# A two-layer graph transformer on one core: graphs taken in pairs, or singly with layer 0 of one beside layer 1 of the one in front

## Chip, core and metric

The kernel runs on one core of a Trainium2 chip. The metric is device time in microseconds. Three runs of the kernel before gave a median of 3158.67 us (3156.97 to 3158.88). A separate profiled execution has a span of 3156.3 us, and all readings of the trace refer to that span.

## What is computed

There are 32 graphs of 512 nodes with 256 features, in float32, each with a 512 x 512 integer adjacency. Two layers follow each other, both with 8 attention heads of 32 features:

```python
# layer 0
allowed = (adj > 0) | (adj.T > 0) | eye
h  = layernorm(x + attention(x, allowed) @ Wo.T + bo) * ln1_g + ln1_b
h  = layernorm(h + relu(h @ W1.T + b1) @ W2.T + b2) * ln2_g + ln2_b   # 256 -> 1024 -> 256
x2 = layernorm(x + h)
# layer 1
out = layernorm(x2 + attention1(x2, adj != 0) @ Wo1.T + bo1)
```

The graphs do not depend on each other. Within one graph everything is a chain.

## The kernel before, in words

One `Graph` object holds the tiles of a graph; its methods each issue a small piece of work, and `period` lists calls of these methods by hand. The order of the calls is the order of the instructions on every engine: the program is built without a scheduler, each engine works through its own queue in that order, and waits on semaphores where an operand or a buffer is not ready. `Absent` objects stand for graphs before the first and after the last: their methods do nothing.

The pieces that matter here:

- `scores` (L279): four matmuls of 32 contraction rows, one per head, into the only score buffer (`ps_s`, four PSUM banks), and the exponential on ScalarE into one of eight `p` tiles. A layer has eight such steps, k = 0 to 7: two head groups times four blocks of keys.
- `masked` (L293): VectorE multiplies `p` with the mask. `product` (L297): TensorE multiplies `p` with the values into 32 output columns a head; after the fourth of a head group ScalarE copies the result to `cT`.
- `pair` (L315) adds two `p` tiles by a DMA that GpSimd issues (p0 += p1, p2 += p3, p4 += p5); `fold` (L320) adds two on VectorE; `sums` (L328) lets TensorE add the folded tile over the keys; `divide` (L346) divides `cT` by it on VectorE, with two small additions on GpSimd in between.
- `project` (L389), then `out0` or `out1` (residual and statistics on VectorE), `root` (L369: add and power on GpSimd, two instructions), and `norm1` or `offset` and `norm4` (on ScalarE).
- The MLP works by halves of the nodes, h = 0 and 1: `hidden` (L408) four times, `mlp` (L434) twice, `out2`, `root(2)`, `norm2` (L446), `root(3)`, `norm3` (L452), which writes the rows of `x2`.
- `transpose` (L237) turns two blocks of 128 rows of `x`, `x1` or `x2` into `xT` through TensorE; `query_key` (L265) and `value` (L249) read `xT`.
- `cast` writes the adjacency to DRAM as bfloat16 (DMA from GpSimd); `entries` reads it back plain and transposed (DMAs from SP); `masks` (L213) makes both masks on VectorE; `load` and `again` bring `x` twice; `residual`, `residual1`, `residual2` add a row to a tile by DMA from GpSimd; `store` writes the result.

One call of `period` in the kernel before takes two graphs, c and d, through layer 0 and the next two steps of their life: first the second half of layer 1 of a pair in front (b's scores), then layer 0 of c, layer 0 of d beside the MLP of c, then layer 1 of c beside the MLP of d. Seventeen calls cover the 32 graphs.

Pools: `ps_d` gives three PSUM buffers in turn to everything but scores and products; products have one bank (`ps_a`); `work` has two buffers per tag unless a line says otherwise (`xT` one, `hT` one, `cT` one, `p` eight, `m1` four).

Of the kernel before, what the change touches and what calls it, by code (L numbers as in the profile page):

```python
# [11 lines left out]
I32 = mybir.dt.int32  # L12
AF = mybir.ActivationFunctionType
# [13 lines left out]
def kernel(ctx: ExitStack, tc: tile.TileContext, t: dict, out: bass.AP):  # L27
# [121 lines left out]
    def plain(pools: ExitStack):  # L149
# [26 lines left out]
        class Graph:  # L176


            def __init__(self, b):
                self.b = b  # L180
                self.mv, self.rs, self.pf = {}, {}, {}
# [7 lines left out]
            def load(self):  # L189
                nc.sync.dma_start(out=self.tile("x", [NQ, D]), in_=x[self.b].rearrange("(c p) d -> p c d", p=P))  # L190

            def again(self):

                nc.sync.dma_start(out=self.tile("x1", [NQ, D]), in_=x[self.b].rearrange("(c p) d -> p c d", p=P))

            def cast(self):

                self.code = hbm.tile([N, N], BF16, tag="code", name=f"code_{self.b}")
                nc.gpsimd.dma_start(
                    out=self.code.rearrange("(p c) k -> p (c k)", p=P),  # L200
                    in_=adj[self.b].rearrange("(p c) k -> p (c k)", p=P),
                )

            def entries(self):

                nc.sync.dma_start(
                    out=self.tile("m0", [NQ, N], BF16), in_=self.code.rearrange("(c p) k -> p c k", p=P)
                )
                self.tile("m1", [NQ, N], BF16, bufs=4)
                for i in range(NQ):  # L210
                    nc.sync.dma_start_transpose(out=self.m1[:, i, :], in_=self.code[:, i * P : (i + 1) * P])  # L211
# [9 lines left out]
            def once(self):  # L221

                if self.b == 0:
                    value_bias(0)
                    graphs[3].masks()
# [11 lines left out]
            def transpose(self, src, h):  # L237

                if h == 0:
                    self.tile("xT", [ND, N], bufs=1)  # L240
# [87 lines left out]
            def sums(self, k, hg, first=False, last=False):  # L328

                if first:  # L330
                    self.total = ps_d.tile([P, N], F32, tag="d", name=f"psR_{self.b}_{hg}")
# [4 lines left out]
                for i in beats:  # L336
                    for j in range(HPC):
                        nc.tensor.matmul(  # L338
                            self.total[j * HD : (j + 1) * HD, :],
# [6 lines left out]
            def divide(self, hg):  # L346
# [3 lines left out]
                nc.vector.transpose(sT.rearrange("p a b -> p (a b)"), self.total)  # L350
# [125 lines left out]
        graphs = [Absent()] * 2 + [Graph(b) for b in range(B)] + [Absent()] * 4  # L476

        def period(a, b, c, d, e, f):

            b.scores(1, 0)
            b.masked(1, 0)
            b.query_key(1, 0, 1)
            b.scores(1, 2)
            b.query_key(1, 1, 1)
            b.scores(1, 1)
            b.masked(1, 2)
            a.sums(3, 1, first=True, last=True)
            a.divide(1)  # L490
            b.product(0)
            d.load()
            c.transpose(c.x, 0)
            b.scores(1, 3)
            c.transpose(c.x, 1)
            a.project(1, 0)
            b.masked(1, 1)
            a.out1(0)
            b.scores(1, 5)
            b.masked(1, 3)  # L500
            b.masked(1, 5)
            a.out1(1)
            d.again()
            b.product(1)
            b.pair(0)
            b.product(2)
            b.scores(1, 4)
            a.project(1, 1)
            b.pair(2)
            a.out1(2)  # L510
            c.query_key(0, 1, 0)
            b.masked(1, 4)
            b.scores(1, 7)
            a.out1(3)
            c.query_key(0, 0, 0)
            b.masked(1, 7)
            b.product(3)
            b.scores(1, 6)
            b.fold(2, 2, 0)
            b.product(4)  # L520
            b.residual2()
            a.root(4, 0, 2)
            b.pair(4)
            c.query_key(0, 1, 1)
            b.masked(1, 6)
            a.root(4, 2, 4)

            c.scores(0, 0)
            b.fold(3, 6, 7)
            c.query_key(0, 0, 1)  # L530
            a.offset(0, 2)
            b.sums(2, 0, first=True, last=True)
            a.norm4(1)
            b.divide(0)
            c.scores(0, 1)
            b.fold(3, 3, 4)
            b.product(5)
            b.product(6)
            c.masked(0, 1)
            c.masked(0, 0)  # L540
            c.once()
            b.product(7)
            c.scores(0, 7)
            c.value(0, 0)
            c.residual()
            b.sums(3, 1, first=True, last=True)
            a.norm4(0)
            b.divide(1)
            c.scores(0, 2)
            c.value(0, 1)  # L550
            d.transpose(d.x, 0)
            c.scores(0, 3)
            c.product(0)
            c.masked(0, 2)
            b.project(1, 0)
            c.scores(0, 6)
            c.masked(0, 3)
            c.product(1)
            b.out1(0)
            a.offset(2, 4)  # L560
            c.product(2)
            d.transpose(d.x, 1)
            c.scores(0, 4)
            c.masked(0, 7)
            b.out1(1)
            c.masked(0, 6)
            c.pair(0)
            a.norm4(3)
            d.query_key(0, 1, 0)
            c.pair(2)  # L570
            c.masked(0, 4)
            c.scores(0, 5)
            c.masked(0, 5)
            a.norm4(2)
            d.query_key(0, 0, 0)
            b.project(1, 1)
            c.fold(2, 2, 0)
            c.product(3)

            d.scores(0, 0)  # L580
            c.once1()
            c.fold(3, 6, 7)
            b.root(4, 0, 2)
            b.offset(0, 2)
            b.out1(2)
            a.store()
            b.out1(3)
            c.product(4)
            c.pair(4)
            c.product(5)  # L590
            c.sums(2, 0, first=True, last=True)
            d.masked(0, 0)
            c.product(6)
            d.scores(0, 1)
            c.divide(0)
            c.fold(3, 3, 4)
            b.norm4(0)
            d.value(0, 0)
            c.product(7)
            d.scores(0, 2)  # L600
            d.query_key(0, 0, 1)
            d.query_key(0, 1, 1)
            d.scores(0, 3)
            b.root(4, 2, 4)
            b.norm4(1)
            d.product(0)
            c.sums(3, 1, first=True, last=True)
            b.offset(2, 4)
            d.masked(0, 1)
            d.masked(0, 2)  # L610
            d.product(1)
            b.norm4(2)
            b.norm4(3)
            c.divide(1)
            d.residual()
            d.masked(0, 3)
            d.scores(0, 4)
            d.value(0, 1)
            d.scores(0, 6)
            c.project(0, 0)  # L620
            c.project(0, 1)
            c.out0(0)
            d.pair(0)
            d.scores(0, 7)
            d.product(2)
            c.out0(1)
            c.root(1, 0, 2)
            c.norm1(0)
            c.norm1(1)
            c.out0(2)  # L630
            d.pair(2)
            d.product(3)
            c.out0(3)
            c.transpose(c.x1, 0)
            d.scores(0, 5)
            c.hidden(0, 0)
            c.hidden(0, 2)
            d.masked(0, 6)
            c.root(1, 2, 4)
            c.norm1(3)  # L640
            d.masked(0, 4)
            c.hidden(0, 4)
            c.norm1(2)
            c.hidden(0, 6)
            d.masked(0, 5)
            d.masked(0, 7)
            d.product(4)
            d.fold(3, 6, 7)
            d.fold(2, 2, 0)
            c.transpose(c.x1, 1)  # L650
            c.residual1()
            c.mlp(0)
            d.pair(4)
            c.mlp(1)
            c.out2(0)
            c.out2(1)
            c.hidden(1, 0)
            c.root(2, 0, 2)
            c.hidden(1, 2)
            c.hidden(1, 4)  # L660
            e.cast()
            c.hidden(1, 6)
            d.sums(2, 0, first=True, last=True)
            c.norm2(0)
            c.norm2(1)
            c.root(3, 0, 2)
            c.norm3(1)
            c.norm3(0)
            d.product(5)
            d.divide(0)  # L670
            c.transpose(c.x2, 0)
            d.fold(3, 3, 4)
            c.mlp(2)
            c.out2(2)
            c.mlp(3)
            c.root(2, 2, 3)
            c.norm2(2)
            d.product(6)
            c.root(3, 2, 3)
            d.sums(3, 1, first=True, last=True)  # L680
            c.out2(3)
            f.cast()
            d.product(7)
            c.norm3(2)
            c.value(1, 0)
            c.query_key(1, 1, 0, 0)
            e.entries()
            d.divide(1)
            f.entries()
# [329 lines left out]
```

## Time and profile before

The durations below are means over the whole execution, from the groups of the page. Instructions that follow each other directly overlap a little, so a row of them takes less than the sum.

| operation | line | engine | count | mean us |
|---|---|---|---|---|
| mask multiplication, p <- p, m | L295 | VectorE | 512 | 2.28 |
| fold, p <- p, p | L322 | VectorE | 189 | 2.29 |
| exponential | L290 | ScalarE | 512 | 1.88 |
| residual add, statistics (two instructions) | L385, L366, L367 | VectorE | 384, 512, 512 | 0.41, 0.43, 0.18 |
| transposes in `divide` | L350, L356 | VectorE | 256 | 0.71 |
| `norm3` | L454 | VectorE | 128 | 0.41 |
| `root`, add and power | L372, L373 | GpSimd | 320 each | 0.60, 0.89 |
| issue of `pair` (landing after 8.7 in the median) | L318 | GpSimd | 189 | 1.06 |
| scores | L286 | TensorE | 4096 matmuls | busy 584.8 in all |
| products | L303 | TensorE | 4096 matmuls | busy 510.4 in all |
| MLP, both steps | L417, L438 | TensorE | 4096 matmuls | busy 914.4 in all |

A float32 matmul shows as two instructions in the trace, a transpose as one. The text `32*128` behind a matmul gives the rows and columns of the array that it uses: scores use 32 rows (four heads side by side), products and sums 32 columns, all else the full 128 x 128.

### The profile page before, as it was taken

The numbers are of one execution on the slowest core, as the hardware profiler recorded it, in microseconds if no ns is written. First come the engines' busy times: TensorE is split into PE (matmuls) and PEld (weight loads), VectorE is DVE, ScalarE is ACT, GpSimd is POOL, SyncE is SP. The second block draws the span as 40 slices with busy tenths as digits, with TensorE's granted clock in tenths as the row PEclk, the third lists the DMA queues.
The fourth block names the chain that finished last, engine by engine and source line by source line (L and its number), as shares of the span: only waits on it lengthen the run. The fifth ranks groups of instructions, "written<-read, shape, count | busy, mean of one in ns | idle before, by whom it ended". The sixth has DMA issues, their size and how long they took to land.

```text
span 3156.3 us, 43843 instructions
## 1 busy us (share of the span) xinstructions
PE 3105.7 (98%) x17466; PEld 1751.6 (55%) x17466; DVE 2673.4 (85%) x3458; ACT 1683.5 (53%) x1921; POOL 895.4 (28%) x1254
## 2 busy tenths in 40 slices
PE   6999999999999999999999999999999999999998
PEld 2655637456474664746547465564655637456473
DVE  4889797897979879798897988979889798897977
ACT  4455464645646456464563645646455464554644
POOL 0232222332322323232232322322223222332322
PEclk8999999999999999999999999999999999999999
DMA  7656556664656647576465665656656556665633
GB/s 185 121 112 124 119 107 127 121 127 107 120 115 132 123 103 135 103 140 127 102 127 109 136 129 104 129 112 124 123 111 127 121 107 127 120 127 107 124 57 68
DMA packets 239876, 374.00 MB, mean 118 GB/s; under 512 B 80176, under 2 KB 214448, under 8 KB 214960
## 3 DMA queue, kind: packets, MB, share of 16 engines
q0 software_dynamic: 95824, 282.09, 49.2%
q1 hardware_dynamic: 143840, 89.03, 10.5%
q8 instruction: 139, 2.28, 0.3%
q14 instruction: 73, 0.60, 0.1%
HBM read 89.01 MB, written 33.55 MB: 39 GB/s over the span
## 4 chain that ended last, share of the span: by engine, by line
PE 89%; ACT 5%; DVE 3%; DMA 1%; SPq 1%; POOL 1%; issue 1%; POOLq 0%; DVEq 0%
PE psS L286 17%; PE psH L417 14%; PE psF L438 14%; PE psA L303 13%; PE psQK_None L273 8%; PE psV L256 6%; PE psO L397 6%; ACT p L290 5%; PE psR L338 4%; PE psQK L273 4%; PE psT L244 3%; DMA p<-p 1%; DVE st L366 1%; DVE x L381 1%; SPq L211 0%
## 5 line engine op out<-in xcount | busy, mean ns | idle before, releaser
L295 DVE TENSOR_TENSOR p<-p,m 128x2048 f32<-128x2048 f32 x512 | 1158.6, 2280 | 80.0 <-ACT p L290 78.2
L290 ACT ACTIVATE p<-psS 128x2048 f32<-128x2048 f32 x512 | 961.7, 1878 | 481.8 <-PE psS L286 379.8
L286 PE MATMUL psS<-qT,kT 32*128 32x512 f32 x4096 | 584.8, 641 | 11.1 <-ACT p L290 3.0
L303 PE MATMUL psA<-p,v 128*32 128x512 f32 x4096 | 510.4, 599 | 0.0
L417 PE MATMUL psH<-xT,w_L_gnn_W 128*128 128x256 f32 x2048 | 460.1, 381 | 0.0
L438 PE MATMUL psF<-w_L_gnn_W,hT 128*128 128x256 f32 x2048 | 454.3, 380 | 0.0
L322 DVE TENSOR_TENSOR p<-p,p 128x2048 f32<-128x2048 f32 x189 | 428.1, 2286 | 10.2 <-DMA p<-p 7.2
L417 PEld LDWEIGHTS psH<-xT,w_L_gnn_W 128*128 128x128 f32 x2048 | 383.9, 190 | 86.0 <-ACT xT L247 24.3
L438 PEld LDWEIGHTS psF<-w_L_gnn_W,hT 128*128 128x128 f32 x2048 | 384.1, 190 | 61.7 <-ACT hT L425 12.1
L372 POOL TENSOR_SCALAR rs<-mv 128x2 f32<-128x2 f32 (+1 forms) x320 | 190.8, 596 | 775.2 <-DVE mv L367 775.2
L425 ACT ACTIVATE hT<-psH,c_L_gnn_b 128x256 f32<-128x256 f32 x512 | 214.6, 470 | 285.9 <-PE psH L417 284.2
L286 PEld LDWEIGHTS psS<-qT,kT 32*128 32x128 f32 x4096 | 160.1, 183 | 312.3 <-issue 136.0
L318 POOL DMA_DIRECT2D p<-p x189 | 195.1, 1059 | 467.9 <-PE psA L303 295.0
L373 POOL TENSOR_TENSOR rs<-rs,neg_half 128x2 f32<-128x2 f32 (+1 forms) x320 | 286.1, 894 | 26.7
L303 PEld LDWEIGHTS psA<-p,v 128*32 128x32 f32 x4096 | 106.3, 109 | 314.9 <-issue 233.7
L273 PE MATMUL psQK_None<-xT,w_L_gnn_Wqkv 128*128 128x512 f32 x512 | 250.3, 618 | 4.7 <-DMA w_L_gnn_Wqkv<-in_L_gnn_Wqkv_dram 4.7
L397 PE MATMUL psO<-w_L_gnn_Wo,cT 128*128 128x256 f32 x1024 | 244.8, 384 | 0.7 <-DVE held L985 0.5
L397 PEld LDWEIGHTS psO<-w_L_gnn_Wo,cT 128*128 128x128 f32 x1024 | 187.9, 190 | 68.2 <-issue 40.6
L353 POOL TENSOR_TENSOR total<-total,sT 128x16 f32<-128x16 f32 x128 | 28.2, 221 | 654.1 <-DVE sT L350 645.1
L313 ACT COPY cT<-psA 128x512 f32<-128x512 f32 x128 | 74.9, 585 | 215.0 <-PE psA L303 206.7
L247 ACT COPY xT<-psT 128x512 f32<-128x512 f32 x192 | 112.1, 584 | 131.3 <-PE psT L244 131.1
L366 DVE BATCH_NORM_STATS2 st<-y 128x6 f32<-128x256 f32 x384 | 164.3, 428 | 13.1
(67 smaller groups left out, 2912.6 us busy)
## 6 DMA issues: line engine op xcount, KB each, us to landing
p<-p POOLq DMA_DIRECT2D x189, 1024.0 KB, 8.7
x<-in_x_dram SPq DMA_DIRECT2D x64, 512.0 KB, 5.3
x<-bov POOLq DMA_DIRECT2D x64, 512.0 KB, 5.8
code<-in_adj_dram POOLq DMA_DIRECT2D x32, 512.0 KB, 6.0
m<-code SPq DMA_DIRECT2D x32, 512.0 KB, 3.9
x<-s_L_gnn_ln_b POOLq DMA_DIRECT2D x32, 512.0 KB, 8.0
x<-s_L_gnn_b POOLq DMA_DIRECT2D x32, 512.0 KB, 6.0
out_dram<-x SPq DMA_DIRECT2D x32, 512.0 KB, 3.5
```

Source lines behind the costliest of these rows:

```text
L273: nc.tensor.matmul(ps, w[:, i, c * P : (c + 1) * P], self.xT[:, i, at], start=(i == 0), stop=(i == ND - 1))
L286: nc.tensor.matmul(s[:, j, :], self.kT[at, hg, kc * P : (kc + 1) * P], self.qT[at, hg, :], start=True, stop=True)
L290: nc.scalar.activation(p, s, AF.Exp, scale=SCALE)
L295: nc.vector.tensor_tensor(p, p, m[:, k % NQ, None, :].to_broadcast([P, HPC, N]), ALU.mult)
L303: nc.tensor.matmul(self.acc[hg][j * HD : (j + 1) * HD, :], self.v[:, kc, h * HD : (h + 1) * HD], self.p[k][:, j, :], start=(kc == 0), stop ...
L322: nc.vector.tensor_tensor(self.p[dst], self.p[a], self.p[b], ALU.add)
L366: nc.vector.bn_stats(st, y)
L373: nc.gpsimd.tensor_tensor(rs, rs, neg_half[:, a:b, None], ALU.pow)
L397: nc.tensor.matmul(ps[:, j, :], self.cT[:, k, at], wo[layer][:, k, :], start=(k == 0), stop=(k == ND - 1))
L417: nc.tensor.matmul(ps[:, j, :], w1[:, c, at], self.xT[:, c, h * 2 * P : (h + 1) * 2 * P], start=(c == 0), stop=(c == ND - 1),)
L425: nc.scalar.activation(self.hT[h][:, f + j, :], ps[:, j, :], AF.Relu, bias=b1[:, f + j : f + j + 1])
L438: nc.tensor.matmul(ps, self.hT[h][:, f, j * P : (j + 1) * P], w2[:, f, :], start=(f == 0), stop=(f == NF - 1))
```

## The change

The methods stay as they were, but for five small things: `load`, `again`, `cast` and `entries` do nothing if they ran before; `total` becomes a dictionary by head group, so that both sums of a graph can be open at once; `once` no longer calls `masks` of the second graph; `m1` has three buffers in place of four; `xT` has the pool's two in place of one.

The list in `period` is new. One call takes one graph on: layer 0 attention of c beside the second MLP half of b, then layer 1 attention of b beside the first MLP half of c, while a's last steps and d's first steps go between. 35 calls cover the 32 graphs. At the start the second x (twice) and its entries are issued on SP behind two weights, ahead of all other weights.

```diff
             def load(self):
-                nc.sync.dma_start(out=self.tile("x", [NQ, D]), in_=x[self.b].rearrange("(c p) d -> p c d", p=P))
+                if not hasattr(self, "x"):
+                    nc.sync.dma_start(out=self.tile("x", [NQ, D]), in_=x[self.b].rearrange("(c p) d -> p c d", p=P))
...
-                self.tile("m1", [NQ, N], BF16, bufs=4)
+                self.tile("m1", [NQ, N], BF16, bufs=3)
...
-                    graphs[3].masks()
...
-                    self.tile("xT", [ND, N], bufs=1)
+                    self.tile("xT", [ND, N])
...
-                    self.total = ps_d.tile([P, N], F32, tag="d", name=f"psR_{self.b}_{hg}")
+                    self.total[hg] = ps_d.tile([P, N], F32, tag="d", name=f"psR_{self.b}_{hg}")
...
-        graphs = [Absent()] * 2 + [Graph(b) for b in range(B)] + [Absent()] * 4
-        def period(a, b, c, d, e, f):
...
+        graphs = [Absent()] * 3 + [Graph(b) for b in range(B)] + [Absent()] * 4
+        def period(a, b, c, d, e):
+            a.product(7)
+            c.scores(0, 0)
+            a.fold(3, 6, 7)
+            c.masked(0, 0)
+            b.hidden(1, 0)
+            b.hidden(1, 4)
+            c.scores(0, 2)
+            a.fold(3, 3, 4)
+            b.hidden(1, 2)
+            c.product(0)
+            a.sums(3, 1, first=True, last=True)
+            a.divide(1)
+            c.masked(0, 2)
+            c.scores(0, 4)
+            b.hidden(1, 6)
+            a.project(1, 0)
+            a.out1(0)
+            a.out1(1)
+            c.scores(0, 1)
+            a.project(1, 1)
+            a.root(4, 0, 2)
+            a.out1(2)
+            a.out1(3)
+            c.masked(0, 4)
+            a.offset(0, 2)
+            b.mlp(3)
+            c.masked(0, 1)
+            a.norm4(1)
+            a.norm4(0)
+            c.scores(0, 3)
+            b.transpose(b.x2, 0)
+            c.once()
+            b.out2(3)
+            b.mlp(2)
+            c.scores(0, 5)
+            c.product(1)
+            c.product(2)
+            c.residual()
+            a.root(4, 2, 4)
+            c.pair(0)
+            b.root(2, 3, 4)
+            c.masked(0, 3)
+            b.out2(2)
+            c.product(3)
+            b.root(2, 2, 3)
+            c.scores(0, 6)
+            c.pair(2)
+            b.norm2(3)
+            b.query_key(1, 0, 0, 0)
+            b.norm2(2)
+            b.root(3, 3, 4)
+            b.root(3, 2, 3)
+            c.product(4)
+            b.norm3(3)
+            c.masked(0, 5)
+            b.norm3(2)
+            c.masked(0, 6)
+            c.scores(0, 7)
+            c.masked(0, 7)
+            c.fold(2, 2, 0)
+            c.fold(3, 6, 7)
+            a.offset(2, 4)
+            b.transpose(b.x2, 1)
+            b.query_key(1, 1, 0, 0)
+            b.value(1, 0)
+            b.query_key(1, 0, 0, 1)
+            c.pair(4)
+            b.query_key(1, 1, 0, 1)
+            b.scores(1, 0)
+            c.product(5)
+            c.fold(3, 3, 4)
+            a.norm4(3)
+            a.norm4(2)
+            c.product(6)
+            c.product(7)
+            c.sums(2, 0, first=True, last=True)
+            b.scores(1, 2)
+            b.query_key(1, 0, 1)
+            c.sums(3, 1, first=True, last=True)
+            c.divide(0)
+            c.divide(1)
+            c.once1()
+            b.scores(1, 1)
+            b.query_key(1, 1, 1)
+            b.residual2()
+            c.project(0, 0)
+            b.scores(1, 5)
+            b.masked(1, 0)
+            c.project(0, 1)
+            c.out0(0)
+            c.out0(1)
+            b.masked(1, 1)
+            c.root(1, 0, 2)
+            b.value(1, 1)
+            c.norm1(0)
+            c.norm1(1)
+            c.out0(3)
+            c.out0(2)
+            b.masked(1, 2)
+            b.scores(1, 3)
+            b.product(0)
+            d.entries()
+            a.store()
+            b.product(1)
+            c.transpose(c.x1, 0)
+            b.pair(0)
+            c.root(1, 2, 4)
+            b.scores(1, 7)
+            c.hidden(0, 0)
+            c.hidden(0, 6)
+            b.masked(1, 3)
+            c.norm1(3)
+            c.norm1(2)
+            b.scores(1, 4)
+            b.product(2)
+            b.masked(1, 5)
+            d.load()
+            b.product(3)
+            d.transpose(d.x, 0)
+            d.again()
+            b.pair(2)
+            c.transpose(c.x1, 1)
+            c.hidden(0, 4)
+            d.transpose(d.x, 1)
+            e.cast()
+            c.residual1()
+            d.value(0, 0)
+            c.hidden(0, 2)
+            d.value(0, 1)
+            b.scores(1, 6)
+            d.query_key(0, 1, 0)
+            c.mlp(0)
+            c.mlp(1)
+            b.masked(1, 7)
+            b.masked(1, 4)
+            b.fold(2, 2, 0)
+            b.masked(1, 6)
+            d.masks()
+            c.out2(0)
+            c.out2(1)
+            c.root(2, 0, 2)
+            c.norm2(0)
+            c.norm2(1)
+            d.query_key(0, 1, 1)
+            d.query_key(0, 0, 0)
+            d.query_key(0, 0, 1)
+            b.sums(2, 0, first=True, last=True)
+            b.product(4)
+            b.pair(4)
+            b.product(5)
+            b.divide(0)
+            c.root(3, 0, 2)
+            c.norm3(0)
+            c.norm3(1)
+            b.product(6)
+        with tc.manual_schedule():
+            first, second = graphs[3:5]
+            first.load()
+            for dst, src in resident[:4]:
+                nc.sync.dma_start(out=dst, in_=src)
+            first.cast()
+            second.cast()
+            first.entries()
+            first.again()
+            for dst, src in resident[4:6]:
+                nc.sync.dma_start(out=dst, in_=src)
+            second.load()
+            second.again()
+            second.entries()
+            for dst, src in resident[6:]:
+                nc.sync.dma_start(out=dst, in_=src)
+            for k in range(-1, B + 2):
+                period(*graphs[k + 1 : k + 6])
...
-            first.cast()
-            second.cast()
-            first.again()
-            first.entries()
-            for dst, src in resident[4:]:
-                nc.sync.dma_start(out=dst, in_=src)
-            second.entries()
-            first.masks()
-            for k in range(-1, B // 2):
-                period(*graphs[2 * k + 2 : 2 * k + 8])
```

## The prediction

> **What bounds it now.** The busy line of the page comes first, then the windows view over the start, two double periods and the end (columns: window, length, busy us and count of PE, PEld, DVE, ACT, POOL; clock; DMA share; GB/s).
>
> ```profile
> PE 3105.7 (98%) x17466; PEld 1751.6 (55%) x17466; DVE 2673.4 (85%) x3458; ACT 1683.5 (53%) x1921; POOL 895.4 (28%) x1254
> ```
> ```profile
> 0.00:79.00 79.00, 51.79 (x248) 20.93 (x248) 37.09 (x28) 32.71 (x29) 7.78 (x18) 0.89 0.79 185
> 79.00:268.16 189.16, 188.59 (x1077) 107.50 (x1073) 162.72 (x213) 100.42 (x114) 54.95 (x76) 1.00 0.61 120
> 268.16:461.91 193.75, 193.20 (x1090) 109.19 (x1089) 167.42 (x217) 105.13 (x120) 55.97 (x79) 1.00 0.61 120
> 461.91:655.66 193.75, 193.19 (x1090) 109.20 (x1089) 167.40 (x217) 105.14 (x120) 56.05 (x79) 1.00 0.61 120
> 2982.16:3156.30 174.14, 159.58 (x914) 95.38 (x914) 129.81 (x195) 79.17 (x98) 44.75 (x69) 0.98 0.34 64
> ```
>
> Two graphs take exactly 193.75 us, 96.88 each, with TensorE idle for 0.55. So an order can win only at the two ends (42 us idle) or inside the busy time. The timeline of TensorE shows what is inside (start, length):
>
> ```profile
> 394.75 1.14 PE L286 MATMUL psS<-qT,kT 32*128 32x512 f32 x8
> 395.82 1.98 PE L273 MATMUL psQK_None<-xT,w_L_gnn_Wk 128*128 128x512 f32 x4
> 397.89 1.14 PE L286 MATMUL psS<-qT,kT 32*128 32x512 f32 x8
> 398.96 1.06 PE L338 MATMUL psR<-p,ones 128*32 128x512 f32 x8
> 399.85 1.04 PE L303 MATMUL psA<-p,v 128*32 128x512 f32 x8
> 400.82 0.66 PE L244 MATMUL psT<-ident,x 128*128 128x128 f32 x4
> 401.40 1.14 PE L286 MATMUL psS<-qT,kT 32*128 32x512 f32 x8
> ```
>
> Comparing starts over all such groups: a full (128\*128) group costs 0.104 more at the head of a run and 0.093 more at its end, a column-tiled (128\*32) one 0.024 and 0.114, a score group (32\*128) always 1.071. Also, scores are 3.14 apart at least (394.75 to 397.89): the one score buffer is free only after the exponential (1.88 us).
>
> **What the Trainium skill says.** "TensorEngine Tiling (Array Packing)", Key Properties: a change of tiling mode drains the array. The trace agrees: 0.20 us per full run, 0.14 per column run. "SBUF — State Buffer", Who interferes with whom: a tensor_tensor with both inputs in SBUF holds off a GpSimd instruction that reads SBUF, and the second one waits. The trace agrees; from its timelines of GpSimd and VectorE:
>
> ```profile
> 251.82 2.16 POOL L372 TENSOR_SCALAR rs<-mv 128x2 f32<-128x2 f32 x1 [1.60 <-DVE mv L367]
> 254.06 2.63 POOL L373 TENSOR_TENSOR rs<-rs,neg_half 128x2 f32<-128x2 f32 x1
> ```
> ```profile
> 251.65 6.66 DVE L295 TENSOR_TENSOR p<-p,m 128x2048 f32<-128x2048 f32 x3
> ```
>
> The two halves of a `root`, 0.22 and 0.57 when free, end only 0.08 and 0.58 us after the mask multiplication in which they began. This prices what follows.
>
> **The change, part by part.** Engine by engine the instructions are the same, only their order differs.
>
> *Mode runs.* A pair of graphs has 184.25 us of groups without switches. Before: 30 full runs (5.9, less 0.4 as nine begin with the cheaper transpose) and 21 column runs (2.9) give 192.6; the score distance adds 1.1: 193.75, as measured. After, per pair: 28 full runs (5.5 less 0.4), 16 column runs (2.2), score waits 0.02: 191.6, or **95.8 a graph if nothing else waits**, 1.08 less.
>
> *A new wait.* I laid VectorE's and GpSimd's queues beside TensorE's starts for one period (t = 0 at `a.product(7)`; a mask multiplication or fold takes 2.20 back to back, one residual with statistics 1.0, `norm2` 1.57, `norm3` 0.33, divide 2.5, all from the timeline). Most due times are met: `a.sums(3,1)` at 9.57 has its fold at 8.6, `project(1,0)` at 13.45 its divide at 13.2. One is not. `b.transpose(b.x2, 1)` falls at 34.82 on TensorE and needs `norm3(2)`. VectorE's queue to there: `a.project(1,1)` ends, 18.30; `out1(2)`, `out1(3)` 20.30; `masked(0,4)` 22.50; offset 22.57; `masked(0,1)` 24.77; `out2(3)` 25.77; `masked(0,3)` 28.0 (its exponential, behind `norm4` on ScalarE, is ready at 25.7); `out2(2)` 29.0; `norm2(3)` 30.57; `norm2(2)` 32.13, its statistics 32.23; `norm3(3)` 32.5 to 32.8. Now `masked(0,5)` starts, and the second half of `root(3,2,3)` (first half 32.33 to 32.55) lands inside it: mask end 34.8 + 0.58 = 35.4, `norm3(2)` 0.41: 35.8, to TensorE 35.9. **TensorE waits 1.0 to 1.3 us; I take 1.1** (1.0 for an undelayed `root(3,3,4)`, 1.3 where the issue of `pair(2)`, 0.9 us, delays it). Behind the waiting transpose stand four query-key groups, a value group and `b.scores(1,0)`, and through them all of layer 1: it is paid in full. VectorE meets the later due times with that shift (`project(0,0)` by 0.4, `transpose(x1,0)` by 0.9, `hidden(0,0)` by 1.1). A graph: **95.8 + 1.1 = 96.9**, as before.
>
> *The start.* Wqkv lands at 11.6 as before; value and query-key of graph 0, 10.3 us plus 2.9 for the half clock until 17.3, bring the first score to 24.9. Graph 0 is alone: eight scores at 3.14 or more (last at 47.7), exponential and mask to 53.0, three folds to 59.6, two divides 64.5, projection 66.4, then residuals, `norm1` and transposes to 76.9; the rest of the period is TensorE's own work, to 98.1. Period 1 lacks `a` (5.6 us less) and takes 90.7: period 2 begins at **188.8**. The earlier x load of the second graph crosses its entries and the later weights on SP. It ends the 15.6 us wait seen for x before, but TensorE needs that x only at 76 here, so the load is hidden; so are the weights of the MLP behind it, due at 72.
>
> *The end.* From the start of period 32: MLP half, `a`'s fold and projection, and the chain to the transpose bring `b.scores(1,0)` to 33.5; eight lone scores to 56.3, exponential 59.4, mask 61.7, products and sums to 67.9. Before, the last sums end at 3139.4 and the span at 3156.3; the same tail gives **84.6**.
>
> *Other edits.* The third m1 and second xT buffer: each tile's last reader is over 10 us before the next writer in the walk. Entries, cast, loads, residual rows move with their graph on SP and GpSimd; `masks(d)`, due at 83, comes 20 us after its entries are issued. The guards and the dictionary of totals issue nothing. `pair(4)`, issued at 94.3, the quickest 7.0 us in the trace: it lands at t = 5.6 of the next period, before its fold at 6.3. At the median 8.7 the sums still come in time; at the 12.4 of the slowest tenth, under contention, they are 3.6 late.
>
> *Sum.* 188.8 + 30 x 96.9 + 84.6 = 3180.4, against a span of 3156.3. The median of the runs shown is 2.4 above that span: **3183 us**.
>
> **Rivals.** (1) *Faster:* the due time at `transpose(b.x2, 1)` is met and the saved switches show in full. For: every other due time I checked is met, and 0.6 us of the wait hangs on which of two instructions begins first. Against: the chain is 17.6 us long where 16.5 is allowed. It decides once that chain is 1.1 shorter. 188.8 + 30 x 95.8 + 84.6 + 2.4 = 3150. (2) *Same:* GpSimd's second half begins outside the mask, as 289 of 320 did in the trace: the wait falls to 0.5, 3165. Against: by my times it comes just after. (3) *Slower still:* a second place goes late, `a.sums(3,1)` behind `pair(4)`. It decides when that landing takes over 8.8 us; each 1 us beyond is 30 us: 3213. Against: no other large transfer is near it. (4) That the order isn't what the diff says: the engines' queues after building show it, so no chance.
>
> **How the numbers follow.** The new wait (3172 to 3194): 0.50. Rival 1 (3142 to 3158): 0.21. Rival 2 (3158 to 3172): 0.13. Rival 3 (3194 and more): 0.16. The two ends, never seen alone, add 8 us either way. The range 3147 to 3210 leaves out under half of each outer case. About 0.2%, 6 us, is what a measurement of this kernel can tell from no change. Faster than 3152: 0.18; to 3165: 0.12; slower: 0.70.
>
> **What would show it.** Right: periods of about 96.9; column runs down from 21 to 16 per pair; on TensorE one idle gap of about 1.1 us per graph before psT, released by L460 (`norm3`); a POOL power of 2.6 us ahead of it. Wrong: periods of 95.8 without that gap (rival 1), or idle before psR or psO released by the fold or the divide (rival 3); a first score of graph 1 far from 98 would fault the start.

## The result, and the profile after

The changed kernel takes **3196.6 us** (median of four runs, 3194.5 to 3199.7) against 3158.3 for the kernel before in four runs beside it. The ratio is 1.0123, with a 95% interval of 1.0105 to 1.0140: 1.2% slower. The profiled execution has a span of 3194.6 us, and all readings below refer to it.

The busy line and the shares of the chain that ended last, from the page after:

```profile
PE 3097.2 (97%) x17466; PEld 1765.7 (55%) x17466; DVE 2666.7 (83%) x3458; ACT 1678.6 (53%) x1921; POOL 1114.6 (35%) x1254
PE 79%; DVE 13%; POOL 3%; DMA 2%; issue 2%; ACT 1%; POOLq 0%; SPq 0%; DVEq 0%
```

The counts are those of before. TensorE is busy 8.5 us less, so its idle time is 97.4 us where it was 50.6. VectorE's work did not grow, yet it now carries 13% of the chain where it carried 3%. GpSimd is busy 219 us longer with the same instructions: the two of `root` (L378, L379) now take 1.03 and 1.26 us on average where they took 0.60 and 0.89, so they are being held.

The windows view, cut at the starts of `a.product(7)`, shows the start, one regular period, the last full one, period 31 (which has no fourth graph) and the tail:

```profile
0.00:204.27 204.27, 166.28 (x833) 92.59 (x837) 120.86 (x150) 81.64 (x92) 39.41 (x60) 0.92 0.61 131
204.27:301.26 96.99, 95.87 (x548) 54.80 (x544) 83.54 (x108) 52.38 (x60) 35.58 (x40) 1.00 0.61 120
2921.91:3018.91 97.00, 95.87 (x548) 54.80 (x544) 83.44 (x108) 52.39 (x60) 34.98 (x39) 1.00 0.53 103
3018.91:3104.71 85.80, 84.69 (x509) 47.90 (x504) 77.87 (x97) 47.49 (x52) 34.65 (x38) 1.00 0.56 105
3104.71:3194.60 89.89, 65.36 (x358) 36.06 (x350) 47.86 (x79) 30.01 (x37) 11.84 (x27) 0.90 0.14 31
```

A graph takes 97.00 us, against 96.88 before, and 1.12 us of it is idle. So the steady part is level, and 32 x 97.0 = 3104.0 leaves 90.6 us of the span for the two ends, where 32 x 96.88 left 56.3. **Of the 38.3 us lost, 34 lie outside the regular periods**: 1.7 of them in two longer periods, treated below, the rest at the two ends, where graph 0 and graph 31 now run with fewer graphs beside them. What the order saved on mode switches in between was taken back by one wait. The timeline of TensorE shows it (start, length; brackets: idle before, and what ended it):

```profile
238.01 1.14 PE L292 MATMUL psS<-qT,kT 32*128 32x512 f32 x8
240.28 0.66 PE L250 MATMUL psT<-ident,x 128*128 128x128 f32 x4 [1.12 <-DVE x L460]
```

And the timelines of GpSimd and of VectorE ahead of it:

```profile
236.74 0.22 POOL L378 TENSOR_SCALAR rs<-mv 128x1 f32<-128x1 f32 x1
237.04 2.73 POOL L379 TENSOR_TENSOR rs<-rs,neg_half 128x1 f32<-128x1 f32 x1
```
```profile
236.47 0.18 DVE L373 BATCH_NORM_AGGREGATE mv<-st 128x2 f32<-128x6 f32 x1
236.74 0.41 DVE L460 TENSOR_SCALAR x<-z,mv,rs 128x256 f32<-128x256 f32 x1
237.06 2.28 DVE L301 TENSOR_TENSOR p<-p,m 128x2048 f32<-128x2048 f32 x1
239.81 0.41 DVE L460 TENSOR_SCALAR x<-z,mv,rs 128x256 f32<-128x256 f32 x1 [0.46 <-POOL rs L379]
```

The power (L379, second line of GpSimd) takes 2.73 us, where such a power mostly takes 0.57 to 0.59 with no mask multiplication (L301) beside it. `norm3(2)` waits 0.46 behind the mask, and the transpose waits for `norm3(2)`. The waits view has this wait once for each graph but one; 29 of the 31 are between 1.11 and 1.13 us (total us, times, longest):

```profile
PE psT L250 <- DVE x L460: 33.5, 31, 1.1
```

### The profile page after: what moved, and what is told of

Its sections match the earlier page's. It is cut to its first block, busy times and chain, and to the rows that moved or that the text cites. A ratio compares the mean times of both kernels' runs of the same rounds, so it can differ in the third digit from the quotient of the medians.

```text
span 3194.6 us, 43966 instructions
## 1 busy us (share of the span) xinstructions
PE 3097.2 (97%) x17466; PEld 1765.7 (55%) x17466; DVE 2666.7 (83%) x3458; ACT 1678.6 (53%) x1921; POOL 1114.6 (35%) x1254
## 4 chain that ended last, share of the span: by engine, by line
PE 79%; DVE 13%; POOL 3%; DMA 2%; issue 2%; ACT 1%; POOLq 0%; SPq 0%; DVEq 0%
PE psH L423 14%; PE psS L292 13%; PE psQK_None L279 11%; PE psA L309 11%; DVE p L301 7%; PE psF L444 7%; PE psO L403 7%; PE psV L262 7%; PE psR L344 4%; PE psT L250 3%; PE psQK L279 3%; POOL rs L379 2%; DVE st L372 2%; DMA p<-p 2%; DVE y L391 1%
## 5 line engine op out<-in xcount | busy, mean ns | idle before, releaser
L301 DVE TENSOR_TENSOR p<-p,m 128x2048 f32<-128x2048 f32 x512 | 1156.1, 2279 | 73.8 <-ACT p L296 73.8
L378 POOL TENSOR_SCALAR rs<-mv 128x2 f32<-128x2 f32 (+1 forms) x320 | 328.3, 1026 | 889.8 <-DVE mv L373 886.7
L423 PE MATMUL psH<-xT,w_L_gnn_W 128*128 128x256 f32 x2048 | 490.2, 388 | 0.7 <-ACT xT L253 0.7
L309 PE MATMUL psA<-p,v 128*32 128x512 f32 x4096 | 486.9, 598 | 3.5 <-DVE p L301 3.5
L379 POOL TENSOR_TENSOR rs<-rs,neg_half 128x2 f32<-128x2 f32 (+1 forms) x320 | 404.5, 1264 | 26.7
L359 POOL TENSOR_TENSOR total<-total,sT 128x16 f32<-128x16 f32 x128 | 38.9, 304 | 798.2 <-DVE sT L356 795.7
L309 PEld LDWEIGHTS psA<-p,v 128*32 128x32 f32 x4096 | 113.4, 109 | 316.0 <-issue 252.5
L324 POOL DMA_DIRECT2D p<-p x189 | 177.2, 941 | 271.8 <-PE psA L309 197.9
L279 PE MATMUL psQK_None<-xT,w_L_gnn_Wqkv 128*128 128x512 f32 x512 | 233.1, 598 | 0.0
L282 ACT ACTIVATE kT<-psQK_None,c_L_gnn_bqkv 128x512 f32<-128x512 f32 x64 | 44.0, 687 | 249.5 <-PE psQK_None L279 249.3
L356 DVE STREAM_TRANSPOSE sT<-psR 128x512 f32<-128x512 f32 x128 | 91.4, 714 | 97.4 <-PE psR L344 93.2
```

What stands on the lines that cost most here:

```text
L279: nc.tensor.matmul(ps, w[:, i, c * P : (c + 1) * P], self.xT[:, i, at], start=(i == 0), stop=(i == ND - 1))
L301: nc.vector.tensor_tensor(p, p, m[:, k % NQ, None, :].to_broadcast([P, HPC, N]), ALU.mult)
L309: nc.tensor.matmul(self.acc[hg][j * HD : (j + 1) * HD, :], self.v[:, kc, h * HD : (h + 1) * HD], self.p[k][:, j, :], start=(kc == 0), stop ...
L378: nc.gpsimd.tensor_scalar(rs, self.mv[n][:, a:b, 1:2], EPS, None, ALU.add)
L379: nc.gpsimd.tensor_tensor(rs, rs, neg_half[:, a:b, None], ALU.pow)
L423: nc.tensor.matmul(ps[:, j, :], w1[:, c, at], self.xT[:, c, h * 2 * P : (h + 1) * 2 * P], start=(c == 0), stop=(c == ND - 1),)
```

## The experiments

Eleven kernels bear on it: the changed one and ten variants of it. Each line of a diff names a call in `period` of the changed kernel, unless it shows other code. Ratios are to the kernel before, which took 3157.0 to 3157.7 beside them.

**1. Take the wait away at its place.** `norm3(2)` goes ahead of the mask multiplication.

```diff
             b.norm3(3)
-            c.masked(0, 5)
             b.norm3(2)
+            c.masked(0, 5)
             c.masked(0, 6)
```

> norm3(2) is put ahead of masked(0,5) on VectorE; nothing else moves. Theory W (the wait of 1.12 us before transpose(b.x2, 1) is a price of its own, as the prediction sums it): the wait goes, 31 x 1.1 = 34 us less than the changed kernel, about 3162. Theory V (VectorE is the bound of the whole stretch from one projection to the next, and the transpose is only where that first shows): the power of root(3) is free, norm3(2) ends at 33.8 in place of 35.9, but masked(0,6) begins when it did before, so that project(0,0), whose operand was ready 0.12 us ahead in the changed kernel, now waits: a new idle gap of 0.8 to 1.0 us before psO, released by the last step of the divide, and only 3 to 10 us less, 3187 to 3194.

It took 3187.4 us, 1.0098 [1.0082, 1.0115], as Theory V has it. The idle time before psT is gone, yet a period is 96.62, not 95.8. The waits view and the timelines of TensorE and VectorE of this variant show where the rest went:

```profile
PE psO L403 <- DVE cT L363: 17.9, 32, 0.9
```
```profile
257.08 0.59 PE L403 MATMUL psO<-w_L_gnn_Wo,cT 128*128 128x256 f32 x2
258.20 1.56 PE L403 MATMUL psO<-w_L_gnn_Wo,cT 128*128 128x256 f32 x6 [0.53 <-DVE cT L363]
```
```profile
239.21 0.41 DVE L460 TENSOR_SCALAR x<-z,mv,rs 128x256 f32<-128x256 f32 x1 [0.49 <-POOL rs L379]
239.53 6.69 DVE L301 TENSOR_TENSOR p<-p,m 128x2048 f32<-128x2048 f32 x3
257.46 0.69 DVE L363 TENSOR_TENSOR cT<-cT,rT 128x512 f32<-128x512 f32 x1
```

The first matmul of psO (two instructions) needs only the first head group; the second needs the second `divide` (L363), which ends at 258.15. From its start to that of the next group psO takes 0.80 us longer than in the changed kernel. How little room VectorE has there is seen in the changed kernel, in the windows view from its first `out1` to the end of that second `divide`:

```profile
219.64:256.57 36.93, 35.81 (x216) 18.47 (x217) 34.16 (x49) 21.84 (x22) 19.84 (x22) 1.00 0.76 155
```

VectorE is busy for 34.16 of 36.93 us, 92.5%. So **VectorE bounds this stretch** of the changed kernel: taking one wait from TensorE there shows the next one.

**2. Fill VectorE's gaps in that stretch.** Two mask multiplications go where VectorE had been idle.

```diff
             a.sums(3, 1, first=True, last=True)
+            c.masked(0, 2)
             a.divide(1)
-            c.masked(0, 2)
...
             a.project(1, 0)
+            c.masked(0, 4)
             a.out1(0)
...
             a.out1(3)
-            c.masked(0, 4)
             a.offset(0, 2)
```

> masked(0,2) is put ahead of a.divide(1), and masked(0,4) ahead of a.out1(0): VectorE does them in the two gaps of 1.95 and 0.9 us in which it waits for the sums and for the projection. Theory V: about 1 us leaves the VectorE stretch that sets the period, the wait at the transpose shrinks to under 0.2 and none comes before psO: 28 to 34 us less than the changed kernel, 3163 to 3169. Theory W says the same, by the earlier end of norm3(2). A rival, N: the masks hold up the divide and the residuals behind them by up to 0.4 and 0.6 us, TensorE waits before psO of layer 1, and the gain is under 15 us.

3174.1 us, 1.0056 [1.0040, 1.0073]: 22.5 us less, short of the 28 expected. The windows view over one of its regular periods:

```profile
1000.00:1096.03 96.03, 95.22 (x543) 54.23 (x542) 83.26 (x107) 51.83 (x61) 30.97 (x39) 1.00 0.60 120
```

The best periods are 96.04, of which about 0.2 us are still the wait before psT; others lie between 96.1 and 96.8, and three at 97.3 to 97.7. Nothing was taken from VectorE (83.3 us a graph here, 83.5 in the changed kernel); work was put where it had been waiting.

**3. Both of these.** 

> Both earlier reorderings in one: masked(0,2) and masked(0,4) in VectorE's gaps, and norm3(2) ahead of masked(0,5). Theory V: with 1 us less of VectorE work in the stretch, the earlier norm3 no longer moves the wait on to the projection; both waits go, the period falls to 95.9, the pure sum of TensorE's groups: 31 x 1.1 = 34 us less than the changed kernel, about 3161 to 3165. If something else has come up to the same due times (GpSimd, the exponentials), the period stays at the 96.1 to 96.2 of the filled kernel alone: 3172 to 3176.

3175.8 us, 1.0064 [1.0048, 1.0079], the same as the second alone. A period is 96.16: no wait before psT, and 0.35 us inside the first psO group. The wait has moved once more to the other end of the stretch. VectorE is not full ahead of it, though. Its timeline has three waits in every regular period:

```profile
611.75 2.29 DVE L301 TENSOR_TENSOR p<-p,m 128x2048 f32<-128x2048 f32 x1 [1.11 <-ACT p L296]
618.97 0.41 DVE L460 TENSOR_SCALAR x<-z,mv,rs 128x256 f32<-128x256 f32 x1 [0.64 <-POOL rs L379]
619.84 0.41 DVE L460 TENSOR_SCALAR x<-z,mv,rs 128x256 f32<-128x256 f32 x1 [0.46 <-POOL rs L379]
```

The first waits for an exponential, the other two for `root(3)` on GpSimd. In experiment 2 the mask multiplication stands between the two `norm3` and covers the 0.46; here nothing does. So the second case of the expectation came true: after the filling, by this trace, the exponentials and GpSimd delay VectorE's last row of masks, folds and divides. No run took these waits away.

**4. What a mode switch is worth.** One product is taken out of its column run and put inside the full run behind it.

```diff
             d.load()
-            b.product(3)
             d.transpose(d.x, 0)
...
             c.hidden(0, 4)
+            b.product(3)
             d.transpose(d.x, 1)
```

> b.product(3) is moved from behind b.product(2) into the long full run after c.hidden(0,4): the same work with one column run and one full run more in each graph. If a switch of the array's mode is a fixed price that nothing hides, 0.14 + 0.20 = 0.34 us a graph, 10 to 11 us more than the changed kernel, about 3207, and no new idle gap on TensorE. If it isn't (the price lies in something that only came along with the switches): no change.

3214.7 us, 1.0183 [1.0166, 1.0200]: 18 us more, not the 10 to 11 expected. A period is 97.46, 0.46 more, or 14 us in 31 of them; the rest lies at the ends and in longer periods. By the starts of the groups 0.29 of it is switches, where 0.34 (one full run at 0.20 and one column run at 0.14) was priced. The other 0.17 is a new wait: the transposes of x1 come earlier relative to the rest and wait for `norm1` (L387, on VectorE). So the price of a run holds within 0.05 us, though the total of this variant confounds it with a wait. That a switch costs is what the Trainium skill states in "TensorEngine Tiling (Array Packing)", Key Properties (it drains the array); the size is from these traces.

**5. The earlier x load.** The second x goes back behind all weights.

```diff
             for dst, src in resident[4:6]:
                 nc.sync.dma_start(out=dst, in_=src)
-            second.load()
-            second.again()
             second.entries()
             for dst, src in resident[6:]:
                 nc.sync.dma_start(out=dst, in_=src)
+            second.load()
+            second.again()
```

> The part of the change named sooner load of the second x is undone alone: its two loads stand behind all weights again. Prediction: TensorE first needs this x at about 80 us, the load lands at about 50, so nothing changes (within 3 us of the changed kernel). A rival: the loads now meet the pair transfers of graph 0, whose landings set the first folds, and hold them up by 2 to 5 us, so that undoing it costs that much; or the weights come sooner, and it gains as much.

3198.5 us, 1.0133 [1.0118, 1.0149]; span 3193.9 against 3194.6. The intervals overlap: the place of that load is worth nothing that could be measured here.

**6. The start: bias rows sooner.** The start of the changed kernel was later than predicted. These are its timelines of TensorE, VectorE and GpSimd there:

```profile
64.97 1.93 PE L344 MATMUL psR<-p,ones 128*32 128x512 f32 x8 [8.62 <-DVE p L328]
69.91 1.93 PE L344 MATMUL psR<-p,ones 128*32 128x512 f32 x8 [3.01 <-DVE p L328]
```
```profile
52.94 2.29 DVE L301 TENSOR_TENSOR p<-p,m 128x2048 f32<-128x2048 f32 x1 [0.85 <-ACT p L296]
62.62 4.49 DVE L328 TENSOR_TENSOR p<-p,p 128x2048 f32<-128x2048 f32 x2 [7.39 <-DMA p<-p]
67.56 2.29 DVE L328 TENSOR_TENSOR p<-p,p 128x2048 f32<-128x2048 f32 x1 [0.45 <-DMA p<-p]
```
```profile
43.40 1.37 POOL L169 DMA_DIRECT2D x<-bov  x1 [40.37 <-DMA c_L_gnn_bk<-in_L_gnn_bk_dram]
44.23 1.84 POOL L169 DMA_DIRECT2D x<-s_L_gnn_ln_b  x1
45.01 2.85 POOL L324 DMA_DIRECT2D p<-p  x2
49.15 0.85 POOL L324 DMA_DIRECT2D p<-p  x1 [1.29 <-PE psA L309]
```

After the last mask VectorE is idle for 7.39 us, and TensorE for 8.62: they wait for the pair transfers. Five adding transfers are issued by GpSimd within 6 us and land one after another, at 49.28, 52.51, 57.52, 62.50 and 67.47. Two of them are bias rows of half the size, ahead of the pairs in GpSimd's queue. The bracket names a weight's load for the first, but that load landed at 44.15, after the issue; what the row needs, the bias `bov` from VectorE (L166), was done at 43.1, since its matmuls stand behind the fifth score in TensorE's order. This variant computes the bias in period -1 and loads the weights for it sooner.

```diff
-                if self.b == 0:
+                if self.b == 0 and not hasattr(self, 'layer'):
                     value_bias(0)
...
             d.query_key(0, 0, 1)
+            d.once()
...
-            for dst, src in resident[4:6]:
+            for dst, src in [*resident[4:6], resident[13]]:
...
-            for dst, src in resident[6:]:
+            for dst, src in [*resident[6:13], *resident[14:]]:
```

> The bias row of layer 0 for graph 0 is made before its first scores, in place of after the fifth, and the row be2 is loaded with Wo and bo: the two row additions on GpSimd, behind which the pair additions of graph 0 stand, can be issued some 15 us sooner. If the folds of graph 0 waited because GpSimd's queue was held by the bias (pairs issued at 45.0 in place of 42): 6 to 11 us less, about 3187. If they waited because the three pair transfers run one after another whenever they begin (landings at 57.5, 62.5, 67.5): under 3 us less.

3195.1 us, 1.0120 [1.0103, 1.0137]: inside the noise of the changed kernel, and under the 3 us of the expectation's second case. The pairs land at 53.41, 59.01 and 63.86, still about 5 us apart, the last 3.6 us sooner, and the first transpose of x1 starts at 77.03 rather than 80.64. But three of graph 0's scores now come 4.09 us apart (12.26 for the three, where the changed kernel took 11.07), since the group takes 2.09 us rather than 1.14: the granted clock is 0.50 from 36 to 48 us, where it was 0.72. The last score starts at 53.98 rather than 49.82, so the last two pairs are issued 4.2 us later than in the changed kernel, and that cuts the gain. Of the 3.6 us, 1.5 are left in the total, too little to tell from none.

**7. The start: no transfers.** For layer 0 of graph 0 the sums are taken over all eight `p` tiles by TensorE, as the kernel already does for layer 1 of the last graph; its three pair transfers and three folds are left out, and the same sums come out.

```diff
-                return self.b == B - 1 and self.layer == 1
+                return (self.b, self.layer) in ((0, 0), (B - 1, 1))
```

> For layer 0 of the first graph alone, TensorE adds all eight p tiles itself (32 matmuls in place of 8), as it does for the last graph; the three pair transfers and the three folds of that graph are left out, the result is the same sum. If the start was mis-sized because the folds waited for the three transfers (8.6 and 3.0 us idle before psR), these waits go, 5 us of matmuls come, VectorE saves 6.6: 9 to 13 us less than the changed kernel, about 3185. If the start is bound by something else (weights, the scores alone), under 4 us less.

The timeline of TensorE in this variant has no gap where there had been 8.62 and 3.01:

```profile
55.46 1.06 PE L309 MATMUL psA<-p,v 128*32 128x512 f32 x8 [2.08 <-DVE p L301]
56.34 7.05 PE L344 MATMUL psR<-p,ones 128*32 128x512 f32 x64
71.67 0.33 PE L250 MATMUL psT<-ident,x 128*128 128x128 f32 x1 [2.24 <-DVE x L387]
```

The transposes of x1 come 9.0 us sooner (71.67 for 80.64), and so does the second MLP half of graph 0, by 9.8. The total falls by 5.4 only, to 3191.2 us, 1.0108 [1.0093, 1.0124]: by the trace 1.6 are lost again within period 1, 1.7 in irregular longer periods, treated below, and 0.9 in the tail. Put on top of experiment 3, which has edits 1 and 2, it gains 9.8 us: **3166.0 us**, 1.0030 [1.0019, 1.0040], the fastest of the variants. The forecast for that kernel was 44 us; it gains 30.6, because the first two edits gave 20.8 together rather than 34.

> The filled kernel, the earlier norm3 and the first graph's sums on TensorE together. If the three terms add up: 34 + 10 = 44 us less than the changed kernel, 3150 to 3156, that is 0.1 to 0.2 per cent under the kernel before. If they overlap, above 3160, and the kernel before stays the fastest.

**8. Ease the other end of the stretch.** On top of that, a score group and two mask multiplications go ahead of `project(0)`, so that `divide` has time.

```diff
             b.residual2()
-            c.project(0, 0)
             b.scores(1, 5)
             b.masked(1, 0)
+            b.masked(1, 1)
+            c.project(0, 0)
             c.project(0, 1)
             c.out0(0)
             c.out0(1)
-            b.masked(1, 1)
             c.root(1, 0, 2)
```

> The kernel with the filled gaps, the earlier norm3 and the first graph's sums, with one step more: b.scores(1,5) goes ahead of c.project(0,0), so that both projections form one full run and the first comes 1.3 us later; masked(1,1) fills VectorE ahead of out0(0). Theory V: the last wait of the stretch, 0.35 us inside psO, goes, a full run is saved (0.20), a score waits 0.15 for the exponential: the period falls from 96.16 to about 95.8, 31 x 0.4 = 12 us less, near 3154, under the kernel before by 0.1 per cent. If the later residuals hold up the transpose of x1 instead, a new wait of 0.3 to 0.8 us stands before that psT and the period stays at 96.1 or more.

3179.3 us, 1.0067 [1.0054, 1.0081]: slower than without it. The timeline of TensorE shows why:

```profile
1020.19 1.98 PE L279 MATMUL psQK_None<-xT,w_L_gnn_Wk 128*128 128x512 f32 x4
1022.95 1.14 PE L292 MATMUL psS<-qT,kT 32*128 32x512 f32 x8 [0.78 <-ACT kT L282]
```

`scores(1,5)` reads the second head group of kT, which the matmuls directly ahead make and ScalarE has to copy out first. The 0.78 us come 32 times, 24.9 us in all, where the changed kernel has one such wait. Nor is a full run saved, as its expectation counts: a regular period has 14, as in the changed kernel. This one was a slip of the variant, and the next takes `scores(1,3)` of the first head group in its place.

```diff
-            b.scores(1, 5)
+            b.scores(1, 3)
             b.masked(1, 0)
             b.masked(1, 1)
...
-            b.scores(1, 3)
+            b.scores(1, 5)
             b.product(0)
```

> The same order as the variant that moves the project groups behind a score group, but with scores(1,3), which reads head group 0, in the place of scores(1,5), and the other way round. If the 0.85 us there were the bias step of kT's second half (TensorE waits for ScalarE), the gap ahead of psS is gone and the period falls from 96.66 to 95.8 to 96.0: 30 periods x 0.75 = 22 us off 3179.3, about 3152 to 3158, level with the kernel before or just ahead of it. If VectorE's stretch is the bound instead, the wait comes back at psO of layer 0 (released by cT), with a period of 96.4 or more and 3170 or above.

3169.5 us, 1.0042 [1.0028, 1.0055]. That wait is gone, and psO has none either, but a period is still 96.18. From the timeline of TensorE:

```profile
2089.61 0.55 PE L250 MATMUL psT<-ident,x 128*128 128x128 f32 x3 [0.59 <-DVE x L387]
```

The mask multiplications put ahead of the projection delay the residuals behind it on VectorE, and the transposes of x1 wait for `norm1`. In a regular period, by the starts of the groups, that costs 0.21 us (up to 0.59 in a few others, as in the line above); 0.15 more is a score held to the spacing of 3.14, as expected. Together they are the 0.37 above 95.81. So this is the third place at which the stretch has shown itself. No variant of the new order reached the kernel before.

## Why the prediction was right, and where its sizes were off

**Mode runs: right.** A regular period has 14 full and 8 column runs, 28 and 16 for two graphs, as forecast. 95.8 us without the wait plus 1.19 us at the group ahead of the transpose (1.12 of it shown as idle) makes the measured 97.0; no other group of a regular period departs from its static cost by as much.

**The new wait: right in place, cause and size.** With t = 0 at 204.27, `norm3(3)` began at t = 32.47 (predicted 32.5), the transpose was due at 34.89 (34.82) and began at 36.0 (35.9). The wait is 1.12, and 1.1 was taken. Experiment 1 confirms the cause: without that order the wait at that place is gone. One reading was mixed up without harm: the powers that end 0.58 behind their mask have two columns (128x2) and take 0.72 when free, not 0.57; the one here has one column, takes 0.57 when free, and ends 0.43 behind the mask.

**What the wait was worth: not asked in the prediction.** Rival 1 has 95.8 as soon as that chain is 1.1 us shorter, since "every other due time I checked is met". Experiments 1, 3 and the last one say otherwise: VectorE meets the next due time, `project(0,0)`, with little to spare, and removing the wait gave 0.38 us a graph, not 1.1. The prediction's 0.4 of slack there was the number to look at. In the changed kernel cT was ready (256.57) 0.12 us before psO began and 0.56 before the first of its instructions that reads cT's second half (257.13). When TensorE comes 1.1 sooner and VectorE does not, all but that slack comes back as a wait: 1.1 less 0.4 is 0.7, and 0.80 was measured.

**The start: mis-sized by +15.5.** Period 2 begins at 204.27, not 188.8. Three terms make it up.
- "Three folds to 59.6" left out their transfers. The prediction priced `pair(4)` against a fold in the steady state, but not the pairs of graph 0: the folds end at 69.8, and the first `hidden` comes at 83.26 rather than 76.9 (+6.4; the divide of the first head group had meanwhile been made). Experiment 7, without the transfers, brings that point 9.3 us forward.
- "TensorE's own work, to 98.1" is 28.1 us and not 21.2 (+6.9). The groups alone are about 25.6 by their steps in a regular period, so my sum was 4.4 short; 2.5 more went to small gaps and to a granted clock of 0.51 in the 6.2 us after the wait.
- Period 1 has its own late pair: landed 10.96 us after its issue, it costs 1.04 us before psR, and 0.97 before psO follows (+2.2 net).

**The periods: +4.5.** 29 of them took 97.06 on average rather than 96.9.

**Period 31: -11.1.** "30 x 96.9" counted it as full, though its fourth graph is absent: it takes 85.8. This is a slip in the count.

**The tail: +5.3.** 89.9 rather than 84.6. The last graph's first score comes at 37.6 rather than 33.5 (+4.1): ahead of it TensorE waits 3.11 for the fold of graph 30 and 5.24 before the last transpose of x2, on chains that nothing stands beside any more. From there to the last sums it takes 36.9, not 34.4 (+2.5), and the end behind them 1.3 less. No experiment changed the tail.

Together 15.5 + 4.5 - 11.1 + 5.3 = 14.2, which is 3194.6 less 3180.4. The range allowed 8 us either way for the ends; the errors were larger and partly cancelled. That is luck: with period 31 counted rightly the sum would have missed by 25 us rather than 14. And 3196.6 lies just above the band of the case that came true (3172 to 3194), in the one kept for rival 3, which is not what put it there: the ends did.

**The load of x: right.** Hidden, by experiment 5. **Rival 2** (the power begins outside the mask) came about in period 10 alone of the regular ones: there the power ran free in 0.59, the wait was 0.80 and the period 96.68. In the others it began about 20 ns before the mask and was held all the same. **Rival 3** happened in two periods instead of thirty, just as it was told: in periods 9 and 20 `pair(4)` landed after 9.2 us, over the 8.8 allowed, and `a.sums(3,1)` (psR) waited 0.8 us. A third such wait, 1.0 us in period 1, is at `c`'s fold.

## What to carry to other kernels

An order that saves work on the bound engine is worth only what the second engine has to spare between its own due times. Add up that engine's work between two of its deadlines, not its share over the span (83% here, but 92.5% in the 37 us that mattered), and with it what it waits for on other engines: removing one wait there shows the next one, 0.38 us for 1.1. And the two ends must be priced as carefully as the period: which graphs are absent, and which transfers lose the work that hid them; here the ends cost some 33 us, and the regular period 0.12 us a graph.

## What the hardware showed that I had not expected

**A power that begins 20 ns first is held, one that begins 75 ns first is not.** The Trainium skill, "SBUF — State Buffer", Who interferes with whom, says for the shared port that the first to issue gets it, and the other one is blocked. Here the power started at 237.04 and the mask at 237.06, and the power took 2.73 us, ending 0.43 after the mask. So it was 29 times in the changed kernel, with the power 18 to 28 ns ahead as the profile records starts. Two powers there were 78 ns ahead, one of them in period 10, and took 0.59:

```profile
1014.22 0.59 POOL L379 TENSOR_TENSOR rs<-rs,neg_half 128x1 f32<-128x1 f32 x1
1014.30 2.29 DVE L301 TENSOR_TENSOR p<-p,m 128x2048 f32<-128x2048 f32 x1
```

In experiment 2 there are 31 powers 74 to 78 ns ahead, all of them free. So for these two instructions the lead that wins lies between 28 and 74 ns of recorded start. The page speaks of the order of issue, which the records don't show; they don't contradict it.

**Adding transfers land one after another.** Three of 1 MB each, issued 1.2 and 2.9 us apart, landed 5.0 us apart (57.52, 62.50, 67.47), while the quickest of all the run's pairs lands after 7.0. The last one was 18.3 us under way. In experiment 6 the first pair had no adding transfer ahead of it, but weights still loading, and took 10.1.

**A slower pair from time to time.** The pair issued at 785.08 landed after 7.04 us, as nearly all in its place do (7.0 to 7.8); those at 882.1 and 1949.8 took 9.2 each, and the periods behind them are 1 us longer. Most of the variants have such periods too, 11 periods apart. What slows these transfers stays open; no run was made for it.
